# Three input buffers in the first layer, and each next image's norm issued among the strips of the image before

## The chip, the cores and the metric

The kernel runs on one core of one Trainium2 chip. The metric is the time of one execution on the device in microseconds (us), lower is better. The program holds four network layers one after the other; the change is in the first stage of the first layer.

## The reference, cut to what matters

The input `x` has 3 images of 256 channels and 48x48 pixels. Each layer adds a convolutional block to a group-normed copy of its input. The first stage of the first block is all that the change touches:

```python
# x: (3, 256, 48, 48)
x = x + _L0_conv_ref(_gn(x), ...)          # layer 0; layers 1 to 3 follow in the same manner

def _gn(v, G=32, eps=1e-5):                # mean and variance over 8 channels and all pixels
    g = v.reshape(B_, G, C_ // G, H_, W_)
    m = jnp.mean(g, axis=(2, 3, 4), keepdims=True)
    s = jnp.var(g, axis=(2, 3, 4), keepdims=True)
    return ((g - m) / jnp.sqrt(s + eps)).reshape(v.shape)

# in _L0_conv_ref
y = conv_bn_silu(x, cv1_w, cv1_g, cv1_b, cv1_m, cv1_v)   # 1x1 convolution 256 -> 256, batch norm, SiLU
y1, y2 = (y[:, :CC], y[:, CC:])                          # CC = 128
cur = y2
for i in range(NB):                                      # two blocks
    a = attention(groupnorm1(cur, ...), ...)             # q, k and v come from images 0, 1 and 2
    ...
```

## The kernel before

The images are processed in the order 2, 1, 0 (`ORDER`). In `xb` an image lies as 128 partitions by two halves (`CT`) of 2304 pixels (`N`); a strip (`chunk`) is 384 pixels (`CH`), and there are six (`NCH`). `xin` is the pool that holds `xb`, with two buffers.

For each image the stage does this:

- It loads the image into `xb` (L456). The first image comes in twelve pieces from the SP and ACT queues, the others in two pieces from SP. Behind the first image SP loads `w0a`, which holds this stage's weights, and behind the second `pj` and `w0b`, for later stages.
- `norm_stats` (L207) runs the generator `norm_steps` (L167) to its end. Its first step makes VectorE's statistics of each strip (`bnst`, L180) and their aggregate (`mv`, L183). The second averages the means over groups of channels by a matmul on TensorE (`ps_gm`, L186), and computes `gm` and `gd` on VectorE (L188 to L192). The third does the same for the variance (`ps_gv`, L195), and takes the inverse root: `ve` on VectorE (L162), a power on POOL (`rstd`, L164).
- VectorE makes the shift `gsh` (L464) and scales this stage's weights by `rstd` into `cv1s` (L467), so that the norm becomes part of the convolution.
- For each strip TensorE multiplies both halves with `cv1s` into PSUM (`ps_y`, L476), for two halves of the output. Right after the first of these, `shifts` computes the bias `ps_b` by four matmuls (L441), and VectorE turns it into `bb` (L445, L446). ScalarE applies the SiLU with `bb` as bias (L482) into `y1` or `cur`. An image has 24 `ps_y` matmuls, each of which leaves two records in the trace, and 12 activations.
- SP stores `y1` and `cur` into `ycat` (L486, L487).

The PSUM pool of the stage, `ps0`, has five buffers, which `ps_y`, `ps_b`, `ps_gm` and `ps_gv` take in turn.

The next stage follows at L953: it norms `cur` of images 2, 1 and 0 with the same `norm_steps` (over all 128 channels, with `mean1` as the matrix), and makes `csc`, `csh` (L504 to L507) and scaled weights `wn` (L568). The values `vt` come from `cur[2]` (`ps_s` at L963, L967), the keys `kt` from `cur[1]` (L592, L596), the queries from `cur[0]` (L725, L753). Then attention begins (L652, L656, L665). `sums` (L557) is a small POOL memset for it.

In this stage the order of the instructions on each engine is not written out by hand: a scheduler orders them by the program's order and what depends on what. From attention on, `keep_order` fixes the order as written.

Of the kernel before, what the change touches and what calls it, by code (L numbers as in the profile page):

```python
# [20 lines left out]
CT = 2  # L21
# [52 lines left out]
ORDER = (2, 1, 0)  # L74
# [10 lines left out]
def net(  # L85
# [43 lines left out]
    gmat = const.tile([P, P], F32, name="gmat")  # L129
# [29 lines left out]
    def rsqrt_eps(var, n):  # L159

        ve = small.tile([P, 2], F32, name="ve")
        nc.vector.tensor_scalar(ve[:, :n], var, 1e-5, None, ALU.add)  # L162
        r = small.tile([P, 2], F32, name="rstd")
        nc.gpsimd.tensor_tensor(r[:, :n], ve[:, :n], mhalf[:, :n], ALU.pow)  # L164
        return r[:, :n]

    def norm_steps(views, mat, psum, tag, stats=None, known=None):  # L167

        n = len(views)
        mv = known
        if known is None:
            mv = small.tile([P, 2, 2], F32, name="mv")
        for i, view in enumerate(views if known is None else ()):
            if stats is None:
                st = small.tile([P, NCH, 6], F32, name="bnst")
                for c in range(NCH):
                    nc.vector.bn_stats(st[:, c, :], view[:, c * CH : (c + 1) * CH])  # L180
            else:
                st = stats[i]
            nc.vector.bn_aggr(mv[:, i, :], st.rearrange("p a b -> p (a b)"))  # L183
        yield
        ps = psum.tile([P, 512], F32, tag=tag, name="ps_gm")
        nc.tensor.matmul(ps[:, :n], mat, mv[:, :n, 0], start=True, stop=True)  # L186
        gm = small.tile([P, 2], F32, name="gm")
        nc.vector.tensor_copy(gm[:, :n], ps[:, :n])  # L188
        d = small.tile([P, 2], F32, name="gd")
        nc.vector.tensor_tensor(d[:, :n], mv[:, :n, 0], gm[:, :n], ALU.subtract)  # L190
        nc.vector.tensor_tensor(d[:, :n], d[:, :n], d[:, :n], ALU.mult)
        nc.vector.tensor_tensor(d[:, :n], d[:, :n], mv[:, :n, 1], ALU.add)  # L192
        yield
        ps2 = psum.tile([P, 512], F32, tag=tag, name="ps_gv")
        nc.tensor.matmul(ps2[:, :n], mat, d[:, :n], start=True, stop=True)  # L195
        rstd = rsqrt_eps(ps2[:, :n], n)
        return mv, gm[:, :n], rstd

    def at_once(steps):

        try:
            while True:
                next(steps)
        except StopIteration as end:
            return end.value

    def norm_stats(*args):  # L207
        return at_once(norm_steps(*args))
# [15 lines left out]
    def chunk(t, c):  # L224
        return t[:, c * CH : (c + 1) * CH]
# [169 lines left out]
    with ExitStack() as l0:  # L395
# [17 lines left out]
        def w(name, at, n):  # L413
            a = W0_AT[name] + at
            if a < W0_SPLIT:
                return w0a[:, a : a + n]
            return w0b[:, a - W0_SPLIT : a - W0_SPLIT + n]
# [12 lines left out]


        with ExitStack() as p1:
            xin = p1.enter_context(tc.tile_pool(name="xin", bufs=2))
            y1p = p1.enter_context(tc.tile_pool(name="y1p", bufs=2))
            ps = p1.enter_context(tc.tile_pool(name="ps0", bufs=5, space=PSUM))

            def shifts(b, sh, bb):
                pb = ps.tile([P, 512], F32, tag="s", name="ps_b1")
                for m in range(2):
                    for ct in range(CT):  # L440
                        nc.tensor.matmul(  # L441
                            pb[:, m : m + 1], w("cv1", ct * 256 + m * P, P), sh[:, ct : ct + 1],
                            start=ct == 0, stop=ct == CT - 1,
                        )
                nc.vector.tensor_tensor(bb, pb[:, :2], b1sc, ALU.mult)  # L445
                nc.vector.tensor_tensor(bb, bb, b1sh, ALU.add)  # L446

            for b in ORDER:
                xb = xin.tile([P, CT, N], F32, name="xb")

                parts = 6 if b == ORDER[0] else 1
                for ct in range(CT):
                    for j in range(parts):
                        at = slice(j * N // parts, (j + 1) * N // parts)
                        queue = nc.scalar if b == ORDER[0] and ct else nc.sync
                        queue.dma_start(xb[:, ct, at], x[b, ct * P : (ct + 1) * P, at])  # L456
                if b == ORDER[0]:
                    nc.sync.dma_start(w0a, w0[:, :W0_SPLIT])
                if b == ORDER[1]:
                    nc.sync.dma_start(pj, projw.rearrange("i p o -> p i o"))  # L460
                    nc.sync.dma_start(w0b, w0[:, W0_SPLIT:])
                _, gm, rstd = norm_stats([xb[:, ct, :] for ct in range(CT)], gmat, ps, "s")
                sh = small.tile([P, CT], F32, name="gsh", bufs=4)
                nc.vector.scalar_tensor_tensor(sh, gm, -1.0, rstd, ALU.mult, ALU.mult)  # L464
                ws = y1p.tile([P, CT, 256], F32, name="cv1s", bufs=2)
                for ct in range(CT):
                    nc.vector.tensor_scalar(  # L467
                        ws[:, ct, :], w("cv1", ct * 256, 256), rstd[:, ct : ct + 1], None, ALU.mult
                    )
                bb = small.tile([P, 2], F32, name="bb")  # L470
                y1 = y1p.tile([P, N], F32, name="y1")
                for c in range(NCH):
                    for m, dst in ((0, y1), (1, cur[b])):
                        pm = ps.tile([P, 512], F32, tag="s", name="ps_y")
                        for ct in range(CT):
                            nc.tensor.matmul(  # L476
                                pm[:, :CH], ws[:, ct, m * P : (m + 1) * P], chunk(xb[:, ct, :], c),
                                start=ct == 0, stop=ct == CT - 1,
                            )
                        if c == 0 and m == 0:  # L480
                            shifts(b, sh, bb)
                        nc.scalar.activation(  # L482
                            chunk(dst, c), pm[:, :CH], AF.Silu,
                            bias=bb[:, m : m + 1], scale=b1sc[:, m : m + 1],
                        )
                nc.sync.dma_start(ycat[b][:, 0, :], y1)  # L486
                nc.sync.dma_start(ycat[b][:, 1, :], cur[b])  # L487
# [1148 lines left out]
    with ExitStack() as l1:  # L1636
        upools[1] = l1.enter_context(tc.tile_pool(name="up1", bufs=1))
        tmp = l1.enter_context(tc.tile_pool(name="tmp", bufs=2))
        ps = l1.enter_context(tc.tile_pool(name="ps1", bufs=5, space=PSUM))
# [155 lines left out]
        for n, (k, h) in enumerate(halves):  # L1795
            layer, b = units[k]
# [37 lines left out]
    with ExitStack() as l3:  # L1834
# [54 lines left out]
        steps = [(at, m, h) for at in range(len(todo)) for m in range(DI) for h in range(2)]  # L1889
# [143 lines left out]
        for s, (at, m, h) in enumerate(steps):  # L2033
            if m == 0 and h == 1 and at + 2 <= last:
                fetch(at + 2)
            for part in range(8):
# [18 lines left out]
                n = busy.get((m, h, part), 0)  # L2055
                if s == 0 and 2 <= part <= 5:
                    n = 3
# [12 lines left out]
                if part == 0 and h == 0:  # L2070
                    c, n = (at, m + 1) if m + 1 < DI else (at + 1, 0)
# [7 lines left out]
                if s == 0:  # L2079
# [17 lines left out]
                    if part in (0, 2, 4):  # L2097
                        ct, lo, hi, t = late_copies[part // 2]
# [73 lines left out]
def net_kernel(tc, *args):  # L2172

    with tc.tile_pool(name="flag", bufs=1) as pool:
        flag = pool.tile([1, 1], I32, name="flag")
        net(tc, *args, flag, False)
        bad = tc.nc.values_load(flag[:1, :1])
        with tc.If(bad > 0):
            net(tc, *args, None, True)
# [79 lines left out]
```

## Time and profile before

| What | Value |
|---|---|
| Median of 3 runs | 3286.74 us (3282.38 to 3290.36) |
| Profiled execution | 3289.23 us |
| Its span, first to last instruction | 3287.5 us |
| Mean granted TensorE clock | 0.989 |
| First convolution begins | 18.21 us |
| Last `ps_y` of the three images ends | about 83.5 us |
| First matmul of attention (`ps_s`, L652) | 109.71 us |
| Statistics of the third image wait for its load | 5.6 us, before 50.43 us |

The page of the profile gives the busy time of each engine over the whole span: TensorE's matmuls 95%, VectorE 87%, ScalarE 73%, POOL 41%. Such shares are averages over stages of quite different kinds. For a change to one short stage the views that count are the stretches of that stage (busy time of each engine between two moments) and the timeline there. In the timeline a row gives the start in us, how long the row lasts, the engine, line and operation, the tiles written and read, how many records are merged in it, and in square brackets the idle time before it and what ended it. "issue" is idle time for which the profile shows no wait.

### The profile page before, as it was taken

To read this page: it belongs to the slowest core of one execution; us is meant where nothing else is said; L and a number is where in the kernel's file an instruction comes from. 1 tells how busy PE (TensorE), PEld (TensorE's weight loads), DVE (VectorE), ACT (ScalarE), POOL (GpSimd) and SP (SyncE) were. 2 spreads that over 40 slices of the span, in tenths; PEclk is the share of its full clock that TensorE was granted. 3 is DMA by queue.
4 is the path that set the end of the run, shared out by engine and by line. 5 is a ranking of instruction groups with operands and counts; after the bars stand their busy time and mean duration, and the time that the engine had idled before them with its cause. 6 is when DMAs were issued, how large, how long until landed. Compare 5 with 4: busy or idle time off the path is not lost.

```text
span 3287.5 us, 54212 instructions
## 1 busy us (share of the span) xinstructions
PE 3123.5 (95%) x20918; PEld 1554.6 (47%) x20918; DVE 2866.2 (87%) x3225; ACT 2392.3 (73%) x3675; POOL 1338.5 (41%) x457
## 2 busy tenths in 40 slices
PE   7999999999999999998999998999999999999996
PEld 4334343363343433556777774444444444444442
DVE  4799989967999899379995449999999999999998
ACT  2688888847888888332323458888888888888885
POOL 0000000000000000121000008999999999999998
PEclk9999999999999999999999999999999999999998
DMA  4000000010000000494631025555555555555552
GB/s 169 32 8 10 5 12 6 8 48 1 8 10 8 9 6 9 136 327 144 227 106 44 34 79 132 138 133 128 133 133 145 139 139 133 128 133 137 143 134 66
DMA packets 182750, 291.14 MB, mean 89 GB/s; under 512 B 34864, under 2 KB 148976, under 8 KB 180560
## 3 DMA queue, kind: packets, MB, share of 16 engines
q1 hardware_dynamic: 169520, 268.69, 30.4%
q10 hardware_dynamic: 12960, 18.88, 1.7%
q8 instruction: 166, 2.72, 0.4%
q14 instruction: 104, 0.85, 0.1%
HBM read 236.40 MB, written 50.64 MB: 87 GB/s over the span
## 4 chain that ended last, share of the span: by engine, by line
PE 55%; DVE 29%; ACT 8%; issue 5%; DMA 2%; POOL 1%; SPq 0%; DVEq 0%; ACTq 0%; POOLq 0%
DVE hs L1968 19%; PE ps_s L652 16%; PE acc L665 15%; PE ps_c L1646 9%; DVE hs L1915 3%; ACT ps_da L1960 3%; PE ps_y L476 2%; PE ps_g L1241 2%; PE ps_m L679 2%; PE ps_m L725 1%; DVE u L296 1%; PE ps_s L1047 1%; PE acc L543 1%; PE ps_s L532 1%; DMA wconv<-in_we 1%
## 5 line engine op out<-in xcount | busy, mean ns | idle before, releaser
L656 ACT ACTIVATE pt<-ps_s 128x1024 f32<-128x1024 f32 x972 | 942.4, 1022 | 154.8 <-PE ps_s L652 142.1
L1968 DVE TENSOR_TENSOR_SCAN hs<-ps_da,hs 128x385 f32<-128x385 f32 x1152 | 1002.4, 934 | 6.9 <-ACT ps_da L1960 5.8
L871 DVE TENSOR_TENSOR part<-part,pt 128x2048 f32<-128x2048 f32 x396 | 906.4, 2289 | 41.3 <-ACT pt L656 18.5
L1960 ACT ACTIVATE ps_da<-dtr,u 128x384 f32<-128x384 f32 x1136 | 642.2, 580 | 116.1 <-DVE hs L1968 105.2
L164 POOL TENSOR_TENSOR rstd<-ve,mhalf 128x2 f32<-128x2 f32 (+1 forms) x25 | 16.0, 640 | 1428.6 <-DVE ve L162 1428.6
L652 PE MATMUL ps_s<-q,kt 32*128 32x512 f32 (+1 forms) x4320 | 576.4, 592 | 0.1
L665 PE MATMUL acc<-pt,vt 128*32 128x512 f32 (+1 forms) x4320 | 521.0, 561 | 0.2
L1646 PE MATMUL ps_c<-vt,u 128*128 128x288 f32 x1728 | 429.8, 409 | 8.7 <-DVE vt L350 8.3
L1976 POOL TENSOR_TENSOR hc<-hs,x 128x3072 f32<-128x3072 f32 x72 | 405.3, 5629 | 8.4 <-POOL hs L1934 4.2
L1976 POOL TENSOR_TENSOR hc<-hs,bc 128x3072 f32<-128x3072 f32 x71 | 400.5, 5641 | 6.8 <-POOL hs L1934 4.4
L1646 PEld LDWEIGHTS ps_c<-vt,u 128*128 128x128 f32 x1728 | 328.9, 191 | 104.1 <-issue 9.1
L652 PEld LDWEIGHTS ps_s<-q,kt 32*128 32x128 f32 x4320 | 195.3, 183 | 199.1 <-issue 120.2
L665 PEld LDWEIGHTS acc<-pt,vt 128*32 128x32 f32 x4320 | 94.4, 108 | 353.4 <-issue 326.7
L1990 PE MATMUL ps_y<-hc,u 128*32 128x384 f32 x2304 | 219.6, 500 | 3.1 <-POOL hc L1976 3.1
L1934 POOL TENSOR_TENSOR hs<-dtur,bc 128x1536 f32<-128x1536 f32 x72 | 210.0, 2916 | 0.0
L1292 PE MATMUL ps_g<-u 128*128 128x384 f32 x576 | 195.3, 492 | 11.7 <-ACT u L1288 11.7
L1934 POOL TENSOR_TENSOR hs<-dtur,x 128x1536 f32<-128x1536 f32 x70 | 203.3, 2904 | 0.0
L1292 PEld LDWEIGHTS ps_g<-u 128*128 128x128 f32 x576 | 108.4, 191 | 95.0 <-ACT u L1288 22.5
L1990 PEld LDWEIGHTS ps_y<-hc,u 128*32 128x32 f32 x2304 | 61.0, 110 | 139.5 <-issue 124.5
L322 POOL MEMSET xpad<- 128x212 f32 x12 | 5.7, 472 | 297.1 <-ACT xpad L1704 226.0
L1669 ACT COPY cb<-ps_c 128x288 f32<-128x288 f32 x48 | 19.2, 401 | 138.8 <-PE ps_c L1646 128.6
L1411 PE MATMUL ps_g<-u 128*128 128x384 f32 x288 | 106.6, 503 | 13.3 <-ACT sz L1419 7.7
(295 smaller groups left out, 4156.1 us busy)
## 6 DMA issues: line engine op xcount, KB each, us to landing
wconv<-in_we SPq DMA_DIRECT2D x144, 384.0 KB, 4.7
dtr<-dtd SPq DMA_DIRECT2D x284, 192.0 KB, 3.7
dtur<-dtud SPq DMA_DIRECT2D x284, 96.0 KB, 4.2
wconv<-xd SPq DMA_DIRECT2D x36, 384.0 KB, 3.8
x<-bcd SPq DMA_DIRECT2D x72, 192.0 KB, 4.7
dtd<-x SPq DMA_DIRECT2D x36, 384.0 KB, 3.0
bc<-bcd SPq DMA_DIRECT2D x72, 192.0 KB, 4.7
dtuq<-dtud SPq DMA_DIRECT2D x284, 48.0 KB, 2.0
```

Source lines behind the costliest of these rows:

```text
L652: nc.tensor.matmul(s[:, j, cols], kt[r, mt * P : (mt + 1) * P], q[r, :n], start=True, stop=True,)
L656: nc.scalar.activation(p[:, h0 : h0 + 2, :], s, AF.Exp)
L665: nc.tensor.matmul(acc[h * HD : (h + 1) * HD, :n], vt[:, mt, g * P + h * HD : g * P + (h + 1) * HD], p[:, h, cols], start=mt == 0, stop=mt ...
L871: ): nc.vector.tensor_tensor(part, first, p, ALU.add)
L1292: nc.tensor.matmul(bank[m % 2], w3v["taps"][:, m, tap, :], w3v["xi"][:, m % 3, tap : tap + CH], start=tap == 0, stop=tap == DCONV - 1,)
L1411: nc.tensor.matmul(bank[j], w("in", ct * 512 + m * P, P), k.xn[:, ct, DCONV - 1 :], start=ct == 0, stop=ct == CT - 1,)
L1646: nc.tensor.matmul(pc[:, :HN], u[:, i, dy, ct, m * P : (m + 1) * P], vt[:, i, ct, dy * TW : dy * TW + HN], start=ct == 0 and dy == 0, stop ...
L1934: nc.gpsimd.tensor_tensor(states(s)[:, :, 2:4, 1:], chunks[at].rows[m][1].unsqueeze(1).broadcast_to([P, 2, 2, CH]), b_rows(s, 0, 2), ALU.mult,
L1960: nc.scalar.activation(slots[n % 3][:, 1 : CH + 1], chunks[at].rows[m][0][:, q, :], AF.Exp, scale=amat[:, col : col + 1],)
L1968: nc.vector.tensor_tensor_scan(b, slots[(8 * s + part) % 3][:, : CH + 1], b, 0.0, ALU.mult, ALU.add)
L1976: nc.gpsimd.tensor_tensor(hc, tiles[s][:, :, :, 1:], cb.broadcast_to([P, 2, 4, CH]), ALU.mult)
L1990: nc.tensor.matmul(k.y_ps[32 * q : 32 * q + 32, :CH], fold, hc[:, g, q, :], start=False, stop=g == 1 and q in ends,)
```

## The change

The pool `xin` gets a third buffer, so that all three images have a place of their own. The body of the image loop that comes ahead of the convolution becomes a generator, `image(b)`, in four parts: the loads; the statistics; `ps_gm` to `gd`; and `ps_gv` to `cv1s`. The first image's generator is run to its end. Those of the other two are then run up to their loads, so that all loads are issued ahead of the first convolution. While an image's six strips are convolved, the next image's generator is advanced by one part ahead of strip 2, of strip 3 and of strip 4. `ready` hands `xb`, `gsh` and `cv1s` to the convolution.

```diff
-            xin = p1.enter_context(tc.tile_pool(name="xin", bufs=2))
+            xin = p1.enter_context(tc.tile_pool(name="xin", bufs=3))
...
-            for b in ORDER:
+            ready = {}
+
+            def image(b):
                 xb = xin.tile([P, CT, N], F32, name="xb")
...
                 if b == ORDER[1]:
                     nc.sync.dma_start(pj, projw.rearrange("i p o -> p i o"))
                     nc.sync.dma_start(w0b, w0[:, W0_SPLIT:])
-                _, gm, rstd = norm_stats([xb[:, ct, :] for ct in range(CT)], gmat, ps, "s")
+                yield
+                steps = norm_steps([xb[:, ct, :] for ct in range(CT)], gmat, ps, "s")
+                next(steps)
+                yield
+                next(steps)
+                yield
+                _, gm, rstd = at_once(steps)
                 sh = small.tile([P, CT], F32, name="gsh", bufs=4)
                 nc.vector.scalar_tensor_tensor(sh, gm, -1.0, rstd, ALU.mult, ALU.mult)
                 ws = y1p.tile([P, CT, 256], F32, name="cv1s", bufs=2)
...
+                ready[b] = xb, sh, ws
+
+            first, *others = (image(b) for b in ORDER)
+            at_once(first)
+            for steps in others:
+                next(steps)
+            for n, b in enumerate(ORDER):
+                xb, sh, ws = ready[b]
                 bb = small.tile([P, 2], F32, name="bb")
                 y1 = y1p.tile([P, N], F32, name="y1")
                 for c in range(NCH):
+                    if c >= 2 and n < len(others):
+                        next(others[n], None)
                     for m, dst in ((0, y1), (1, cur[b])):
```

The matmuls, statistics and activations are the same in number and size; what changes is where they stand and when the third image is loaded.

## The prediction

> **What bounds the kernel now.** I read the chain that ended last first. `ps_y`, the first layer's convolution, holds 2% of it, so a microsecond saved there is a microsecond of the end; but 2% of 3287 us is some 66 us, and no more than that can be touched.
>
> ```profile
> PE 55%; DVE 29%; ACT 8%; issue 5%; DMA 2%; POOL 1%; SPq 0%; DVEq 0%; ACTq 0%; POOLq 0%
> DVE hs L1968 19%; PE ps_s L652 16%; PE acc L665 15%; PE ps_c L1646 9%; DVE hs L1915 3%; ACT ps_da L1960 3%; PE ps_y L476 2%; PE ps_g L1241 2%; PE ps_m L679 2%; PE ps_m L725 1%; DVE u L296 1%; PE ps_s L1047 1%; PE acc L543 1%; PE ps_s L532 1%; DMA wconv<-in_we 1%
> ```
>
> Then the busy times in stretches, cut at the three convolutions (first column) and the handovers between them.
>
> ```profile
> core 0: us, PE busy (x) PEld busy (x) DVE busy (x) ACT busy (x) POOL busy (x), PEclk, DMA share, GB/s
> ...
> 18.20:39.10 20.90, 20.89 (x58) 12.75 (x58) 6.53 (x17) 7.37 (x11) 0.00 (x0) 1.00 0.12 49
> 39.10:42.10 3.00, 0.49 (x5) 0.36 (x4) 1.32 (x8) 0.67 (x1) 0.69 (x1) 1.00 0.95 393
> 42.10:58.70 16.60, 16.59 (x58) 10.24 (x58) 7.47 (x19) 7.37 (x11) 0.00 (x0) 1.00 0.56 214
> 58.70:62.70 4.00, 1.05 (x7) 0.86 (x6) 3.53 (x14) 0.67 (x1) 0.69 (x1) 0.79 0.98 406
> 62.70:83.50 20.80, 20.79 (x58) 12.70 (x58) 6.11 (x18) 7.37 (x11) 0.00 (x0) 0.79 0.09 35
> 83.50:85.80 2.30, 0.15 (x3) 0.09 (x2) 1.32 (x7) 1.95 (x2) 1.00 (x2) 1.00 0.94 385
> 85.80:110.00 24.20, 24.19 (x118) 14.60 (x122) 11.96 (x33) 5.37 (x7) 1.09 (x2) 1.00 0.19 70
> ```
>
> Inside a convolution TensorE is the bound: it is busy throughout, ScalarE a third to nearly half of the time. Between them it is idle 2.5 us (39.1 to 42.1) and 3 us (58.7 to 62.7). The third convolution takes 20.8 us for what the second does in 16.6, at a granted clock of 0.79. The timeline says why the handovers stall.
>
> ```profile
> 38.95 0.28 PE L186 MATMUL ps_gm<-mv,gmat 128*128 128x2 f32 x2
> 40.16 0.35 PE L195 MATMUL ps_gv<-gd,gmat 128*128 128x2 f32 x2 [0.93 <-DVE gd L192]
> 42.11 1.53 PE L476 MATMUL ps_y<-xb,cv1s 128*128 128x384 f32 x4 [1.59 <-issue]
> ...
> 60.77 0.35 PE L195 MATMUL ps_gv<-gd,gmat 128*128 128x2 f32 x2 [1.93 <-DVE gd L192]
> 61.69 0.56 PE L186 MATMUL ps_gm<-mv,mean 128*128 128x1 f32 x2 [0.57 <-DVE mv L183]
> 62.71 2.90 PE L476 MATMUL ps_y<-xb,cv1s 128*128 128x384 f32 x4 [0.47 <-issue]
> ```
>
> The next image's `ps_gm` stands in TensorE's order behind the last `ps_y`, and from there a chain runs with nothing beside it: four small VectorE operations, `ps_gv`, `ve`, POOL's power (0.69 us), `gsh`, `cv1s`. In the second handover VectorE also puts four statistics of `cur` (0.55 us each) between the links. The last column pair is the clock: four records of `ps_y` take 1.53 us at 42.11 and 2.90 us at 62.71.
>
> **The change part by part.** The order in which the built program's instructions stand is the evidence for what moves. Attention and all that follows are unchanged on every engine, so the account ends at about 110 us.
>
> *Handover, image 2 to 1.* `ps_gm` now stands after 12 of the 24 `ps_y`, `ps_gv` after 16, `cv1s` is due at the end. The 3.00 us go. In their place the two pairs of small matmuls run in the stream: bounded by 0.35 us a pair (the row at 40.16) and by 0.14 (from the start of `ps_gm` at 88.46 to the next `ps_s` at 88.60); I take 0.2. Saved: 3.0 − 0.4 = 2.6 us.
>
> *Handover, image 1 to 0.* The same: 4.0 − 0.4 = 3.6 us.
>
> *Clock.* With no pause before it the third convolution should cost what the second does: 20.8 − 16.6 = 4.2 us. [...] In the row, the clock falls to 0.50 at 61 us although the longest pause of TensorE there is 1.93 us, cut off by `ps_gv`. [...] I take the row: the fall lies inside the handover, and the record of `ps_y` is twice as long right after it. [...]
>
> *The end of the stage gets worse.* Before, `ps_gm` of `cur[2]` ran at 61.69 and only `ps_gv` was left after the last `ps_y`. In the new order both stand behind it. From `ps_gm` to `ps_gv` takes 1.2 us (38.95 to 40.16). Given back: the last statistic of `cur[0]`, 0.55 us, leaves its place between `csc` and `csh` (84.72), some 0.35 us of the path; in its new place, before `ve`, it runs while `ps_gv` does. Net cost 0.9 us.
>
> *Loads.* The 2.36 MB of image 0 are issued at about 10.5 us rather than 40.3, on SP behind `w0b` and ahead of `vb` and the `ycat` stores. The queue had drained by 21 us; at the 400 GB/s of 12 to 20 us the load adds 6 us, so it lands near 27 us. `vb`, landing at 22 before, moves to about 28; its reader is at 87. The stores of image 2 lose a rival. The new loads come after `xb` of image 2 and `w0a` in the queue, so the start at 18.2 should stay. Should they instead share the engines equally with image 1, that image's statistics end near 33 us instead of 26.7, `ps_gm` is due near 31.3, and 2 us are lost; I take nothing. Nothing gains from it beyond the handovers already counted.
>
> *New waits.* On VectorE two statistics of `xb` image 0 stand before `ve` of image 1, and one before its `cv1s`. They wait for that load; landed at 27, they are ready when VectorE reaches them at 32.4. From there: two statistics to 33.5; `ps_gv` at 34.1; `ve`, a statistic, power, `gsh`, `cv1s` to 36.3. TensorE wants it at 39.5: cover 3.2 us. Next, `bb` of image 1 waits behind eleven statistics and two aggregations, about 43.0 where `ps_b` is ready at 41.8; ScalarE starts late, but five PSUM buffers let TensorE go on to the fifth tile (45.6). In image 0's turn `gd` follows a `cur[1]` statistic, `cv1s` is ready near 53.2, wanted near 56.5: cover 3.3 us. Its `bb` stands behind the last `cur[1]` statistic (57.5), before `ps_b` is ready (58). If a cover were gone, the excess would go on the path one for one. POOL's order is unchanged, and `sums` still waits for the last `ps_y`. The larger `xin` moves the later pools' addresses: `pt` now waits for two `ycat` stores which land near 77 us, some 20 us before its use.
>
> *Sum.* 2.6 + 3.6 + 4.2 − 0.9 = 9.5 us, against the profiled execution: 3289.23 − 9.5 = 3279.7. That execution stands 2.5 us above the median of the runs, 3286.74; the forecast is 3286.7 − 9.5 = 3277.2 us, 0.29% less. About 0.2%, 6.6 us, is what a measurement can tell from no change.
>
> **The rivals.**
>
> *Clock falls elsewhere.* The new end handover is about 3.2 us (2.3 + 0.9) with only two tiny pairs in it, much like 39.1 to 42.1 (no fall) but not far from 58.7 to 62.7 (a fall). Unknown cost: between nothing, the nearer row, and the 4.2 us that the fall cost the third convolution; I take nothing, and the projections at 85.8 would show it, being TensorE-bound throughout. Or the timed runs of before often had no fall at 61 us. Either leaves 5.3 us: 3281.4. For: one row falls, a similar one doesn't. Against: the pause that fell is the longest, and it goes. 16%.
>
> *It doesn't do what it says.* VectorE's order delivers `cv1s` as late as before, because the dealt steps sit behind statistics. To cancel the 9.5 us both covers (3.2 and 3.3) would have to be overrun and the clock would fall again. Time 3286. Against: the order shows one to three statistics per link. 6%.
>
> *Slower: the third load blocks VectorE.* The statistics of image 0 stand at VectorE's front at 32.4, with `ve` and `cv1s` of image 1 behind. For: in before the same kind of wait on `xb` did hold VectorE 5.6 us, at 50.4, with nothing urgent behind it. It decides from a landing at 35.6 us (cover used up); each further microsecond is one of the end, and from 45 us on the whole gain is lost. Landing at 55 gives 3286.7 − 9.5 + 19.4 = 3296.6. Against: that would take under 100 GB/s over 21 to 45 us, where the rows of loading show about 400. 8%.
>
> **How the numbers follow.** The likeliest case (3277.2) has 70%; of it 63 points lie beyond 0.2% and 7 within, since run-to-run spread (3282.4 to 3290.4) blurs a gain of 0.29%. The clock case: 7 faster, 9 within. The third: 5 within, 1 slower. The load: 8 slower. Together faster 0.70, within 0.2% 0.21, slower 0.09. Range: below the sum 2 us for a fall of the clock at 39 us in runs of before and smaller in-stream costs, and 4 for the spread: 3271. Above, the clock case plus its spread: 3286. What is left out is most of the load case and the tails.
>
> **What would show it.** Right: the three `ps_y` stretches follow each other from 18.2 to about 73 us with no pause over 0.5 us, the second and third near 17 us; the first `ps_s` (L963 before) near 76.3; that stage's clock 1.00. Wrong: VectorE idle on `DMA xb` after 30 us; `ps_y` waiting for `cv1s`; the clock below 1 between 70 and 85 us; or the start of the first convolution later than 18.2.

## The result, and the profile after

| | before | after |
|---|---|---|
| Median of 7 runs each | 3287.34 us | 3278.24 us |
| Range of the runs | 3279.83 to 3290.99 | 3273.97 to 3281.37 |
| Profiled execution | 3289.23 us | 3275.68 us |
| First matmul of attention in it | 109.71 us | 99.38 us |

The ratio is 0.9969, with a 95% interval of 0.9959 to 0.9979: the change makes the kernel 0.31% faster. The forecast was 3277.2 us.

First the busy times of the new kernel in stretches, cut at the starts of its three convolutions, at the handover behind the last, and at the next stage (columns as in the prediction).

```profile
core 0: us, PE busy (x) PEld busy (x) DVE busy (x) ACT busy (x) POOL busy (x), PEclk, DMA share, GB/s
...
18.20:39.60 21.40, 21.40 (x62) 13.14 (x63) 13.14 (x38) 7.74 (x12) 0.69 (x1) 1.00 0.41 170
39.60:56.60 17.00, 17.00 (x62) 10.56 (x61) 7.89 (x24) 8.18 (x13) 0.69 (x1) 1.00 0.34 140
56.60:73.20 16.60, 15.91 (x57) 9.73 (x55) 4.55 (x13) 8.26 (x14) 0.50 (x1) 1.00 0.36 151
73.20:76.40 3.20, 1.31 (x5) 0.97 (x6) 1.94 (x9) 1.20 (x1) 0.55 (x1) 1.00 1.00 415
76.40:101.00 24.60, 24.60 (x124) 14.27 (x122) 11.67 (x31) 6.54 (x8) 1.09 (x2) 1.00 0.10 39
```

TensorE is busy without a break from 18.2 to 72.4 us; the two handovers are gone, and the third convolution runs at a clock of 1.00. (The stretches follow the forecast; the last convolution ends 0.8 us ahead of the boundary at 73.20.) The timeline of TensorE in the same execution shows the handovers one by one.

```profile
30.85 0.28 PE L186 MATMUL ps_gm<-mv,gmat 128*128 128x2 f32 x2
30.99 2.83 PE L494 MATMUL ps_y<-xb,cv1s 128*128 128x384 f32 x8
33.65 0.28 PE L195 MATMUL ps_gv<-gd,gmat 128*128 128x2 f32 x2
33.79 6.70 PE L494 MATMUL ps_y<-xb,cv1s 128*128 128x384 f32 x20
...
57.96 14.44 PE L494 MATMUL ps_y<-xb,cv1s 128*128 128x384 f32 x44
72.23 0.28 PE L186 MATMUL ps_gm<-mv,mean 128*128 128x1 f32 x2
73.34 0.38 PE L195 MATMUL ps_gv<-gd,mean 128*128 128x1 f32 x2 [0.83 <-DVE gd L192]
75.47 0.88 PE L981 MATMUL ps_s<-wn,cur 128*128 128x384 f32 x2 [1.75 <-DVE csh L525]
```

`ps_gm` and `ps_gv` of image 1 stand inside image 2's convolution, without idle time before them; the next `ps_y` starts 0.14 us after each. At the end both matmuls of `cur[2]`'s norm stand behind the last `ps_y`, and only there TensorE still waits. From `ps_s` (L981, which was L963) to the start of attention takes 23.91 us; before it was 23.90. So all that attention gained was gained ahead of `ps_s`.

### The profile page after: what moved, and what is told of

Same layout as the page of the kernel before. It is cut to its first block, busy times and chain, and to the rows that moved or that the text cites. A ratio compares the mean times of both kernels' runs of the same rounds, so it can differ in the third digit from the quotient of the medians.

```text
span 3273.9 us, 54207 instructions
## 1 busy us (share of the span) xinstructions
PE 3120.2 (95%) x20918; PEld 1553.2 (47%) x20918; DVE 2866.4 (88%) x3225; ACT 2392.8 (73%) x3675; POOL 1339.5 (41%) x457
## 4 chain that ended last, share of the span: by engine, by line
PE 56%; DVE 28%; ACT 9%; issue 4%; DMA 2%; POOL 1%; SPq 0%; ACTq 0%; DVEq 0%; POOLq 0%
DVE hs L1986 19%; PE ps_s L670 16%; PE acc L683 15%; PE ps_c L1664 9%; DVE hs L1933 3%; ACT ps_da L1978 3%; PE ps_s L1065 2%; PE ps_g L1259 2%; PE ps_m L697 2%; PE ps_y L494 2%; PE ps_m L743 1%; PE acc L561 1%; DVE u L296 1%; PE ps_s L550 1%; DMA wconv<-in_we 1%
```

## The experiments

All are kernels of the first stage alone; the order of the instructions from attention on stays. "Attention" is the start of the first attention matmul in the profiled execution. Ratios are against the kernel before, with 95% intervals. The first convolution itself begins anywhere from 17.5 to 18.4 us in these executions (26.86 in the one marked *), so a difference of less than a microsecond in the attention column isn't the kernel's.

| kernel | attention, us | median, us | ratio |
|---|---|---|---|
| before, two executions | 109.71, 109.58 | | |
| changed, two executions | 99.38, 102.18 | 3278.24 | 0.9969 [0.9959, 0.9979] |
| early load only | 108.76 | 3286.53 | 0.9993 [0.9986, 1.0000] |
| dealt, two buffers | 115.91 | 3290.23 | 1.0006 [0.9999, 1.0013] |
| first handover only, two executions | 99.16, 98.91 | 3275.62 | 0.9968 [0.9957, 0.9980] |
| second handover only | 105.67 | 3284.24 | 0.9987 [0.9980, 0.9993] |
| before, with a filled handover | 105.99 | 3284.96 | 0.9992 [0.9983, 1.0000] |
| values' norm dealt as well | 96.72 | 3274.40 | 0.9957 [0.9943, 0.9970] |
| and a warm start | 102.82 * | 3280.99 | 0.9980 [0.9973, 0.9986] |
| and a warm start, ordered | 92.68 | 3271.06 | 0.9943 [0.9929, 0.9956] |

### Early load only

```diff
             for n, b in enumerate(ORDER):
+                if n:
+                    at_once(others[n - 1])
                 xb, sh, ws = ready[b]
...
-                    if c >= 2 and n < len(others):
-                        next(others[n], None)
```

> Three buffers and all loads ahead of the first convolution as in the changed kernel, but each next image's norm is issued as a whole after the convolution before it. Theory (the pauses between the convolutions are the cost, and they come from ps_gm standing behind the last ps_y): the first handover stays at 3.0 us, the second at 3 to 4 us, the third convolution runs at a fallen clock again (20.8 us). In this order the norm of cur[2] stands in the second handover, so the end handover should shrink from 2.3 to about 0.9 us. Attention begins near 108 us (109.7 before, 99.4 after); time against before 0.9990 to 1.0000. Rival (the early load of the third image is what pays): attention begins near 100 us, ratio near 0.997.

The early load by itself pays next to nothing (108.76 us, 0.9993); the rival, which had attention near 100 us, falls. The second handover took 3.25 us and the clock fell in it, as the theory had it (the four records of `ps_y` behind it take 2.90 us, at 0.50), and the end handover vanished altogether. But the first was forecast wrong: it took 4.3 us instead of 3.0, and the clock fell there too (2.80 us for the four records). VectorE's part of the timeline shows why.

```profile
38.06 0.16 DVE L188 COPY gm<-ps_gm 128x2 f32<-128x2 f32 x1 [6.65 <-PE ps_gm L186]
38.14 0.55 DVE L180 BATCH_NORM_STATS2 bnst<-xb 128x6 f32<-128x384 f32 x1
38.61 0.14 DVE L190 TENSOR_TENSOR gd<-mv,gm 128x2 f32<-128x2 f32 x1
38.67 0.56 DVE L180 BATCH_NORM_STATS2 bnst<-cur 128x6 f32<-128x384 f32 x1
39.14 0.14 DVE L191 TENSOR_TENSOR gd<-gd 128x2 f32<-128x2 f32 x1
```

With image 0 loaded early, the scheduler has statistics at hand and puts one of some 0.55 us behind each link of the chain.

### Dealt, with two buffers

```diff
-            xin = p1.enter_context(tc.tile_pool(name="xin", bufs=3))
+            xin = p1.enter_context(tc.tile_pool(name="xin", bufs=2))
...
-            for steps in others:
-                next(steps)
+            next(others[0])
             for n, b in enumerate(ORDER):
+                if n == 1:
+                    next(others[1])
                 xb, sh, ws = ready[b]
```

> The norms are dealt over the strips as in the changed kernel, but with two buffers, so that image 0 is loaded only when the convolution of image 2 has ended (near 39 us). Theory (the third buffer is needed, because the dealt statistics and ps_gm stand in the middle of image 1's convolution): the load lands at 50 to 53 us as in the kernel before, mv is ready near 57, TensorE stops after 12 of 24 ps_y of image 1 from about 47.5 to 57, and the clock falls behind the pause. 9 to 10 us of pause and some 4 us of clock take the gain back: attention begins at 111 to 114 us, ratio against before 1.000 to 1.002. Rival (the load is hidden anyway): attention begins near 99.5 us, ratio 0.997.

The mechanism is the expected one: the first statistic of image 0 runs at 51.0 us, and TensorE stops in the middle of image 1, here in its timeline.

```profile
41.53 6.70 PE L495 MATMUL ps_y<-xb,cv1s 128*128 128x384 f32 x20
57.88 0.56 PE L186 MATMUL ps_gm<-mv,gmat 128*128 128x2 f32 x2 [9.65 <-DVE mv L183]
58.30 5.47 PE L495 MATMUL ps_y<-xb,cv1s 128*128 128x384 f32 x8
```

The pause is 9.65 us, and eight records take 5.47 us behind it where 2.83 is the full clock's. Attention begins at 115.91 us, later than the 111 to 114 expected, because the clock fell to 0.50 at the end of the stage too (the first `ps_s` pair takes 1.62 us, in the changed kernel 0.88). In this execution the gain of the first handover is more than used up; the medians (1.0006) can't be told from the kernel before. So the third buffer earns next to nothing by itself (the run of the early load) and is what the dealing needs.

### One handover at a time

```diff
 # first handover only; the other kernel has n == 1 and others[0] in place of these
             for n, b in enumerate(ORDER):
+                if n == 2:
+                    at_once(others[1])
...
-                    if c >= 2 and n < len(others):
+                    if c >= 2 and n == 0:
```

> Only image 1's norm is dealt over image 2's strips; image 0's norm is issued as a whole after image 1's convolution. Theory: the first handover is gone (2.7 us saved), the second stays at 3 to 4 us, the clock falls in it and the third convolution takes 20.8 us, the end handover is about 0.9 us as the norm of cur[2] stands in the second. Attention begins near 105 us; ratio 0.9987. Rival (the fall of the clock at 61 us had nothing to do with the pause): the third convolution takes 16.6 us or any other one 20.8, attention begins near 101 us.

> Only image 0's norm is dealt over image 1's strips; image 1's norm is issued as a whole after image 2's convolution. Theory: the first handover stays at 3.0 us without a fall of the clock, the second is gone (3.7 us), the third convolution takes 16.6 us (4.2 us saved), the end handover is 3.1 us (0.8 lost). Attention begins near 102.4 us; ratio 0.9978. Rival (the clock falls by itself, not by the pause): the third convolution stays at 20.8 us and attention begins near 106.6 us, ratio 0.999.

Both missed. With the first handover alone the kernel is as fast as with both (0.9968 and 0.9969); the second alone (0.9987) brings about two fifths of that. The timeline of the first-handover kernel shows two reasons.

```profile
55.25 0.28 PE L186 MATMUL ps_gm<-mv,gmat 128*128 128x2 f32 x2
55.39 0.36 PE L186 MATMUL ps_gm<-mv,mean 128*128 128x1 f32 x2
56.55 0.35 PE L195 MATMUL ps_gv<-gd,gmat 128*128 128x2 f32 x2 [0.80 <-DVE gd L192]
56.77 0.36 PE L195 MATMUL ps_gv<-gd,mean 128*128 128x1 f32 x2
58.50 1.53 PE L496 MATMUL ps_y<-xb,cv1s 128*128 128x384 f32 x4 [1.37 <-issue]
```

The norm of `cur[2]` (`mean`) rides in the second handover beside image 0's. So that pause of 3.25 us replaces the changed kernel's end pause of 3.24, and there is one pause either way. And the clock didn't fall: 1.53 us for four records. The second handover alone leaves two pauses, 4.3 us and 3.25, and in its execution the clock fell in both (2.80 us for the four records of `ps_y` behind the one, 1.62 for the `ps_s` pair behind the other).

### The clock: a filled handover, and second executions

```diff
 # the kernel before, for image 0: six matmuls of 128x384 in all, whose product nobody reads
-                _, gm, rstd = norm_stats([xb[:, ct, :] for ct in range(CT)], gmat, ps, "s")
+                    next(steps)
+                    next(steps)
+                    fill_pe(3, xb)
+                    rest = at_once(steps)
+                    fill_pe(3, xb)
```

> The kernel before with six extra matmuls of 128x384 in the second handover, whose product nobody reads: three between ps_gm and ps_gv of image 0, three between ps_gv and its first ps_y. The handover stays as long as it was (about 4 us) or grows by some tenths; in the order that comes out, both matmuls of cur[2]'s norm stand behind the last ps_y, so the end handover is 3.1 instead of 2.3 us. Theory (the clock falls because TensorE pauses): the third convolution takes 16.6 us instead of 20.8, and attention begins near 106.4 us. Rival (the fall isn't the pause's): it stays at 20.8 us and attention begins near 110.6 us.

The stretches of the second convolution, of the filled handover, and of the third:

```profile
41.50:58.20 16.70, 16.64 (x59) 10.31 (x59) 7.53 (x19) 7.38 (x11) 0.00 (x0) 1.00 0.55 213
58.20:62.40 4.20, 4.20 (x15) 2.46 (x16) 3.78 (x15) 0.67 (x1) 0.69 (x1) 1.00 0.98 406
62.40:79.00 16.60, 16.60 (x59) 10.18 (x57) 5.56 (x13) 7.28 (x11) 0.00 (x0) 1.00 0.09 39
```

The handover is no shorter (4.45 us from `ps_gm` to the first `ps_y`, before 4.15), but TensorE is busy in it, and the third convolution takes 16.6 us. It was the pause that cost the 4.2 us. Attention begins at 105.99 us, 106.4 expected; in the medians the gain is at the edge of what can be told (0.9992, interval 0.9983 to 1.0000). Whether the same pause always costs this was asked of three kernels by a second execution (3286.03, 3282.07 and 3278.39 us).

> The kernel before, once more, for a second look at the clock in its handovers. Theory A (the pause decides the fall alone): the clock stays full over the first handover (3.0 us) and falls in the second (4.0 us) as in the first profile; attention begins near 109.7 us. Theory B (the same pause falls in some executions and not in others): one of the two handovers differs from the first profile; attention begins at 105 to 106 us with no fall, or later than 111 with two.

> The changed kernel once more. Its three convolutions have no pause and stay at the full clock by both theories; the question is its end handover of 3.1 us. Theory A (a pause of 3.1 us doesn't fall): attention begins near 99.4 us as in the first profile. Theory B (it falls in some executions): if it does here, the first matmul of the values takes 1.6 us instead of 0.9 and attention begins at 100.5 to 103 us.

> The kernel with only image 1's norm dealt, once more. Its second handover of 3.2 us didn't fall in the first profile, and attention began at 99.2 us. Theory A (the length of the pause decides): the same again. Theory B (it falls in some executions): if it falls here, the third convolution takes 18 to 21 us and attention begins at 101 to 103.5 us.

The kernel before fell in its second handover again (2.90 us for the four records behind it), and the first-handover kernel again did not (1.53). The changed kernel differed from its first execution: the clock fell at the end, to 0.50. Its timeline, and its stretches from 70 us on:

```profile
72.16 0.28 PE L186 MATMUL ps_gm<-mv,mean 128*128 128x1 f32 x2
73.27 0.38 PE L195 MATMUL ps_gv<-gd,mean 128*128 128x1 f32 x2 [0.83 <-DVE gd L192]
75.41 1.62 PE L981 MATMUL ps_s<-wn,cur 128*128 128x384 f32 x2 [1.76 <-DVE csh L525]
```

```profile
73.00:76.00 3.00, 0.97 (x3) 0.80 (x4) 2.04 (x10) 1.31 (x2) 0.55 (x1) 0.73 1.00 415
76.00:79.00 3.00, 3.00 (x6) 1.60 (x5) 0.56 (x1) 0.00 (x0) 0.00 (x0) 0.50 0.71 295
79.00:82.00 3.00, 3.00 (x8) 1.81 (x8) 1.44 (x5) 0.00 (x0) 0.00 (x0) 0.63 0.00 0
```

The pause is the same to 0.01 us (72.16 to 75.41, against 72.23 to 75.47), yet the first `ps_s` pair takes 1.62 us instead of 0.88, and attention begins 2.8 us later. Counted over all profiles, behind the start of the first convolution, from the first small matmul of a pause (or the start of idling) to the first large one:

| pause | fell | where |
|---|---|---|
| 2.4 us | 0 of 2 | end, before |
| 3.15 to 3.25 us | 4 of 11 | first handover before (none of 3, one with the second filled); second handover of early load (fell) and of first handover only (none of 2); end of the others (3 of 5) |
| 4.15 us and more | 5 of 5 | second handover before; first of early load and of second only; dealt with two buffers |

By length alone the pauses of 3.15 to 3.25 us look like a draw. The clock records in the traces, which give the time of each change, decide it. In all 13 executions, every stretch at one granted clock between two recorded changes lasts a whole multiple of 3.41 us: at half clock 10.24 us in the kernel before (61.05 to 71.29), 6.83 us in the changed kernel's second execution (74.38 to 81.20). So in these executions the clock changed only on a grid of 3.41 us, which lay differently in each. In the following table the pauses are divided along that grid, and the matmuls of one or two columns (`ps_gm`, `ps_gv`, `ps_b`) are counted as idle.

| kernel and period, us | TensorE idle in it | clock at its end |
|---|---|---|
| changed, 70.75 to 74.17 | 1.77 us | stays |
| changed, second execution, 70.96 to 74.38: the same pause | 2.05 us | falls |
| first handover only, 53.86 to 57.27 | 1.86 us | stays |
| early load only, 59.24 to 62.65: the same pause | 2.29 us | falls |
| before, first handover, 40.57 to 43.98 | 1.88 us | stays |
| before, second handover, 57.63 to 61.05 | 2.33 us | falls |

Over all executions up to 112 us, the clock fell at the end of each of the ten periods with 2.04 us of idle time or more, and of none with 1.96 us or less. With the small matmuls counted as busy the order is lost: a fall at 1.38 us, none at 1.61. (The ends of matmuls are modelled, so the border isn't known more finely than this, and it isn't one for other stages: at 1384.9 us the clock of the changed kernel fell behind a period with 1.28 us of idle time.) A fall costs 1.4 to 4.7 us here (second handover only at its end; early load in its third convolution).

### What was left: the end handover and the cold start

The first of these kernels deals the norm of `cur[2]` over image 0's strips.

```diff
-            first, *others = (image(b) for b in ORDER)
+            def norm_of_values():
+                yield
+                steps = norm_steps([cur[2]], mean1, ps, "s")
+                next(steps)
+                yield
+                next(steps)
+                yield
+                _, gm, rstd = at_once(steps)
...
+                early_norm[0, 2] = sc, sh
+
+            first, *others = [image(b) for b in ORDER] + [norm_of_values()]
```

> The changed kernel with one thing more: the norm of cur[2] for the values (statistics, ps_gm, ps_gv, csc, csh) is dealt over image 0's strips in the same manner, so that the end handover has only wn and the last activation left. Theory: the end handover falls from 3.1 us to about 0.8 (the first ps_s needs the PSUM bank of the last activation, 0.7 us after the last ps_y); attention begins near 97.1 us instead of 99.4, ratio against before 0.996. Rival (VectorE or ScalarE holds the start of that stage anyway): the first ps_s starts no earlier against the last ps_y than 2 us.

Attention began at 96.72 us (97.1 expected): the first matmul of the next stage follows the last `ps_y` directly, and the granted clock is given as 1.00 from 0 to 110 us. What is left of the stage's slowness is the first convolution: 20.9 us from its start to the next one's, where the second takes 16.8. In the kernel before it begins with four records that take nearly twice the 1.53 us of the second convolution:

```profile
18.21 2.93 PE L476 MATMUL ps_y<-xb,cv1s 128*128 128x384 f32 x4 [1.54 <-DVE cv1s L467]
```

> The kernel of the values' norm dealt, and besides 46 matmuls of 128x128 whose product nobody reads, 36 of them on TensorE while it waits for the first image (from about 2.5 us on) and 10 between ps_gm, ps_gv and the first ps_y. Theory (the pause, or here the idle start, sets the clock): the clock is full when the first convolution begins, which then takes about 16.9 us instead of 20.9; the start moves by no more than 0.5 us; attention begins near 93 us, ratio against before 0.995. Rival (the slow first convolution has another cause, such as the loads running beside it): it stays near 21 us and attention begins near 97 us.

This one went wrong in an instructive way. TensorE's timeline of its start:

```profile
14.19 0.38 PE L186 MATMUL ps_gm<-mv,gmat 128*128 128x2 f32 x2 [2.00 <-DVE mv L183]
14.43 1.14 PE L460 MATMUL ps_f<-gmat 128*128 128x128 f32 x8
23.72 0.58 PE L195 MATMUL ps_gv<-gd,gmat 128*128 128x2 f32 x2 [8.15 <-DVE gd L192]
```

The extra matmuls had changed the scheduler's order on VectorE: it put eleven statistics of image 1 ahead of image 2's `gm`, and VectorE waited for image 1's load and then ran them. The clock fell in that gap (the four records of `ps_y` at 26.86 us take 2.74), so the run doesn't answer its question on the first convolution; it shows what work queued in front of a short chain costs. The next kernel ties each image's statistics behind `cv1s` of the image before in VectorE's order.

```diff
+                mark = len(listed)
                 next(steps)
+                for ins in listed[mark:] if scaled else ():
+                    if ins.engine == mybir.EngineType.DVE:
+                        tc.add_manual_dep(ins, scaled[-1], ...)   # order alone
```

> The warm start again (54 matmuls of 128x128 that nobody reads: 44 ahead of the first image's ps_gm, 4 between ps_gm and ps_gv, 6 ahead of ps_y), on top of the dealt norms of images 1, 0 and of the values; now the statistics of each next image stand behind cv1s of the image before in VectorE's order, so that the first image's gm and gd no longer wait behind statistics of images that are still being loaded (8.15 us in the run before). Theory (an idle start sets the slow clock of the first convolution): the first convolution starts near 18 us and takes 16.9 us instead of 20.9; attention begins near 93 us, ratio against before 0.9945. Rival (it is slow for another cause, such as the loads beside it): it takes near 21 us and attention begins near 97 us.

```profile
2.39 12.61 PE L460 MATMUL ps_f<-gmat 128*128 128x128 f32 x88 [2.39 <-POOL gmat L136]
14.84 0.28 PE L186 MATMUL ps_gm<-mv,gmat 128*128 128x2 f32 x2
14.98 1.14 PE L460 MATMUL ps_f<-gmat 128*128 128x128 f32 x8
15.96 0.38 PE L195 MATMUL ps_gv<-gd,gmat 128*128 128x2 f32 x2
16.20 1.58 PE L460 MATMUL ps_f<-gmat 128*128 128x128 f32 x12
17.93 1.53 PE L552 MATMUL ps_y<-xb,cv1s 128*128 128x384 f32 x4
```

In its timeline the first convolution starts at 17.93 us at the full clock (1.53 us for four records, 2.93 in the kernel before), and the next one follows at 34.83: 16.9 us, as expected. The loads are issued as in the changed kernel, where they move 421 GB/s on average from 18 to 26 us; so they weren't the cause, and the idle start was. Attention begins at 92.68. By trace and by median (3271.06 us, ratio 0.9943) this is the fastest kernel; its interval, 0.9929 to 0.9956, lies below the changed kernel's and overlaps that of the values' norm dealt.

## Why the prediction was right, point by point

- **The two handovers.** Predicted 2.6 and 3.6 us. From the start of one convolution to the start of the next it is 21.02 us (before 23.90) and 16.82 (20.60): 2.9 and 3.8. A pair of small matmuls cost 0.14 us in the stream and not 0.2, which is 0.1 of each difference.
- **The clock, 4.2 us.** Right (4.3), and the row was the right one to follow: with the pause filled and nothing shortened, the third convolution took 16.6 us. The clock fell in pauses of 3.25 us, cut by small matmuls, in which the longest idle piece was at most 1.76 us; 2.04 us of idle time in a period of 3.41 was enough, the small matmuls counted as idle. The clock records show the grid of 3.41 us, and the table above shows it dividing equal pauses differently where one falls and the other does not.
- **The end, −0.9 us.** From the end of the last `ps_y` to `ps_s` it is 3.07 us after (72.40 to 75.47), 2.27 before: −0.8. The rival of a clock that falls here came true in one of the two profiled executions, at 2.8 us; with it came one of the prediction's own signs of being wrong, a clock below 1 between 70 and 85 us. The prediction took nothing for it, so its sum of 9.5 us holds for an execution in which the grid spares this pause, and that is luck.
- **The sum.** Attention began 10.3 us earlier in the first execution of the changed kernel, 7.5 in the second (102.18 against 109.71). The 10.3 are 2.9 + 3.8 + 4.3 − 0.8, and 0.2 by which the first convolution happened to begin earlier, within rounding. The medians moved by 9.1 us, between the two; with runs of one kernel 7 to 11 us apart, that it is so near to 9.5 doesn't test the single terms. Of the 13.6 us between the two spans, 3.3 lie behind the start of attention, where the order of both kernels is the same; no cause in the change is known for them.
- **Loads and new waits.** The loads had ended by 28 us (27 predicted for image 0), and no statistic of image 0 waited for its load: VectorE reached them at 31.8 us (predicted 32.4). `cv1s` of image 1 was ready at 35.7, wanted at 39.0: cover 3.3 us (3.2). `bb` of image 1 ran at 41.3 us, right behind `ps_b`, and not at 43.0 as predicted; that delay didn't come. The slower rival did not come about in this kernel; the run with two buffers shows its price when the load is late, and the first warm start shows VectorE's order doing the same.
- **What it missed.** It took each handover as worth its own microseconds. The single-handover runs show they aren't separate: the scheduler puts the norm of `cur[2]` into the second handover when that is left, and dealing only the first norm was as good as dealing both.

## What to carry to other kernels

Between dense matmul phases look at the number of pauses as well as their length: here 9 of the 16 pauses of 3.15 us and more cost a slow restart on top (1.4 to 4.7 us), tiny matmuls in between didn't prevent it, and in the one run that had them six of 128x384 did. One profile doesn't tell whether a pause is safe, as the same pause fell in one execution and not in another (the end of the changed kernel, 3.25 and 3.24 us). When a reorder removes a stall, look at which later chain used that stall as its cover, and deal that too. A scheduler may put ready bulk work between the links of a short chain, as this one did: check the order of the engine that computes the chain, not of the one that waits.

## What the runs showed of the hardware that was not expected

- In this stage the clock changed only on a grid of 3.41 us that lay differently in each execution, and fell where a period had 2.04 us of idle time or more (ten of ten; none at 1.96 or less), matmuls of one or two columns counted as idle. By length of the pause: 4 of 11 fell at 3.15 to 3.25 us, none of 2 at 2.4, 5 of 5 at 4.15 and more.
- The profile gives the granted clock as 1.00 from 18.2 to 39.1 us, yet four records of `ps_y` take 2.93 us there, as at 0.50 later. The first clock record of that trace begins at 26.9 us, and ahead of it the column doesn't show a cold start; the duration of equal matmuls does. With the warm start, ordered, the first record begins at 7.7 us and the four records take 1.53.
